# A two-layer relational graph network on one core: bases multiplied over four chunks at once, and rows copied by hand on one DMA queue in place of two

## The chip, the core and the metric

One core of a Trainium2 chip runs the whole kernel in one launch. The metric is device microseconds for that launch. The engines named below are PE (TensorE; its weight loads are listed apart as PEld), DVE (VectorE), ACT (ScalarE), POOL (GpSimd) and SP (SyncE). SP and ACT can each issue plain DMAs on a queue of their own, and POOL issues indirect DMAs (gathers). An engine runs its instructions strictly in the order of its program, DMA issues included.

## What is computed

There are N = 50,000 nodes with 128 features and 850,000 edges, sorted by target node; 50,000 of them are loops of a node to itself. An edge has one of 16 relations, and the weight of a relation is a mix of 8 bases. Two layers of

```python
W = jnp.einsum('rb,bio->rio', w_comp, basis)
agg = jax.ops.segment_sum(h[src], dst * N_REL + rel, num_segments=N_ENT * N_REL).reshape(N_ENT, N_REL, -1)
msg = jnp.einsum('nri,rio->no', agg, W)
h = relu(msg + h @ loop_w + bias)
```

are followed by `layernorm(x + h)`. All is float32.

## The kernel before, in words

**Chunks.** The 800,000 edges that are not loops are cut into tiles of 128 edges, and K = 10 tiles make a chunk: C = 625 chunks in a layer, 1,250 in all. A chunk's targets lie in a run of some 80 successive nodes. The outer loop (line 876) runs over the layers and the loop at line 940 over the chunks. The program is unrolled completely; the order of PE, POOL, DVE and ACT is the order in which the Python code emits instructions, and the order of SP is left to the planner of the framework.

**Gathers.** For a tile, POOL issues one indirect DMA (line 204, called at 950) that fetches 128 source rows of 512 bytes into one of GATHERS = 5 chunk buffers `g`. The first gather of a chunk waits until PE has read the last tile of the chunk five earlier (`read_by`, lines 951 to 957). Gathers of chunk c + 2 are emitted in chunk c, but POOL is an engine of its own and runs as far ahead as the buffers let it.

**Rows by hand.** In chunks with c % 5 = 4 one tile, and in chunks with c % 5 = 1 one other tile, is not gathered by POOL. Its 128 rows are copied one by one, each by a plain DMA of 512 bytes whose address comes from a register (`row_by_row`, line 814, the DMA at 836). SP copies the tile of the first kind and ACT that of the second (`HANDS`, line 806). The register values are loaded 32 at a time (line 828). Copying begins six chunks before the tile is used and is spread over 45 steps, one after nearly every product, so that two to three row copies at a time stand between the other instructions in ACT's program. Eight semaphores serve the plain DMAs of both queues in turn, so a row copy waits for the DMA that had its semaphore eight copies before, on whichever queue that was.

**Products.** For each tile PE multiplies the 128 gathered rows by a one-hot matrix `hot` that sums them per base and per node slot (12 slots, line 979), into PSUM `pa`, five tiles to a bank. DVE copies each full bank to SBUF (`aT`, line 987). Two chunks later `slots` (line 728) multiplies `aT` of one chunk by the eight bases (line 732: eight matmuls with 120 columns of `aT` as the stationary side and 128 columns moving), and DVE spreads the sum over the J = 4 places of a group row (line 737). Three chunks later `to_nodes` (line 757) adds the result into a group of 512 nodes in PSUM (`pn`, line 768).

**Groups.** There are 98 groups of 512 nodes in a layer, one in 6.4 chunks. For each, `from_itself` (line 681) loads the group's own rows (`h_own`, SP), transposes them on PE (line 695), has ACT copy the result to SBUF (`hT`, line 699), multiplies by the bases (line 710), and lets DVE weigh and reduce (lines 717, 725). The loop weights `lw` come from `loop_weights` (line 644) for four groups at a time, again through a copy on ACT (line 678). At the end of a group `finish` (line 785) adds, applies relu or the normalization on DVE and ACT (lines 792, 587, 595), and SP stores. `weights` (line 619) loads relations for four chunks through SP (`rel`, line 623), which DVE compares at line 630. `beside` (line 916) hands out these pieces between the ten products of a chunk.

Of the kernel before, what the change touches and what calls it, by code (L numbers as in the profile page):

```python
# [50 lines left out]
P = 128  # L51
EPR = 850000
ROW = 10
# [19 lines left out]
SP_EVERY = 5  # L73
ACT_EVERY = 5
OFFSETS = 32
EPS = 1e-5
# [7 lines left out]
def tile_rgcn_resnorm(  # L84
# [33 lines left out]
    assert D == P and N >= P and edges.shape[0] == 1 and AT * NR == P and PER * NB * WN <= BANK and AT * PER * NB == WEIGHTS and PER == HALF and S <= P and C >= 4 and M > 0 and N % C == 0 and N % J == 0 and J * D == BANK and RUN - LK // 2 == LIVE and 2 * C <= NG * P and N <= 1 << 16 and E % ROW == 0  # L118
# [10 lines left out]
    ROW_AT = dram.tile([2 * C, 2, P], I32, name="ROW_AT")  # L129
# [310 lines left out]
    def rows_of(j, pool):  # L440
# [18 lines left out]
        def put(of, to):  # L459
# [17 lines left out]
        row_at = pool.tile([P, LIVE], F32, name="real").bitcast(I32)[:, : 2 * P]  # L477
        nc.vector.tensor_scalar(
            row_at[:m], srcf[:m, LIVE - 2 * P :], float(N - 1), float(4 * D), op0=OP.min, op1=OP.mult
        )  # L480
        nc.sync.dma_start(ROW_AT[r0 : r0 + m].rearrange("r t e -> r (t e)"), row_at[:m])
# [63 lines left out]
    def count_up(pool):  # L545
        last = 5 * NG + len(ROWS)
        off = pool.tile([1, C], F32, name="off_all")
        even = pool.tile([1, C], F32, name="even")
# [48 lines left out]
    def chunked():  # L597
        with (
# [7 lines left out]

            def nodes(g):
                return min(GN, N - g * GN) // J
# [10 lines left out]
            def weights(c, n):  # L619
# [9 lines left out]
                is_rel = hp.tile([P, LIVE], F32, name="is_rel")  # L629
# [14 lines left out]
            def loop_weights(g, n):  # L644
# [14 lines left out]
                is_rel = hp.tile([P // 2, 2, P, J], F32, name="is_l", bufs=1)  # L659
                for h in range(2):  # L660
                    nc.vector.tensor_scalar(  # L661
                        is_rel[:m, h].rearrange("k p j -> k (p j)"), rel[:m, h, :], its_rel1[:m], None, op0=OP.is_equal
                    )
                    if h == 0:
                        yield
                po = ps_o.tile([P, BANK], F32, name="po")
                of = po[:, : J * T * NB].rearrange("p (j t) -> p j t", j=J)
                for j in range(J):
                    for h in range(2):
                        nc.tensor.matmul(  # L670
                            of[:, j, :],
                            is_rel[:m, h, :, j],
                            EACH[n][:m, :T, :].rearrange("k t b -> k (t b)"),
                            start=h == 0,
                            stop=h == 1,
                        )
# [4 lines left out]
            def from_itself(g, of, n):  # L681

                m = nodes(g)
                h = sb.tile([P, J, D], F32, name="h_own", bufs=2)
# [43 lines left out]
            def slots(c, k, aT, n):  # L728

                ps = ps_s.tile([P, BANK], F32, name="ps")  # L730
                for b in range(NB):
# [4 lines left out]
                st = sb.tile([P, J, D], F32, name="slots")  # L736
                nc.vector.tensor_tensor(  # L737
                    st[: k * WN],
                    ps[: k * WN, None, :D].to_broadcast([k * WN, J, D]),
                    which[: k * WN, c, :, None].to_broadcast([k * WN, J, D]),  # L740
                    op=OP.mult,
                )
                yield st
# [61 lines left out]
            behind = {}  # L805
            HANDS = ((nc.sync, SP_EVERY, SP_EVERY - 1), (nc.scalar, ACT_EVERY, ACT_EVERY // 2 - 1))

            def by_hand(c):

                if ks(c) < K:  # L810
                    return []
                return [i for i, (_, every, at) in enumerate(HANDS) if c > every and c % every == at]

            def row_by_row(i, c, of):

                engine, every, _ = HANDS[i]
                tile_at = 1 - by_hand(c).index(i)
                row_at = hp.tile([1, P], I32, name=f"row_at{i}", bufs=2)
                nc.sync.dma_start(row_at, ROW_AT[2 * c + 1 : 2 * c + 2, tile_at])
                to = hp.tile([P, D], F32, name=f"by_hand{i}", bufs=2)  # L820
                byte = of.bitcast(U8).rearrange("n d -> (n d)")
                yield to
                steps = every * (K - 1)
                for step in range(steps):
                    for e in range(step * P // steps, (step + 1) * P // steps):
                        if e % OFFSETS == 0:
                            with tc.issue_after(behind[i]) if i in behind else ExitStack():
                                _, offsets = nc.values_load_multi_w_load_instructions(  # L828
                                    row_at[:, e : e + OFFSETS],
                                    engines=[engine.engine],  # L830
# [5 lines left out]
                        behind[i] = engine.dma_start(row, byte[None, ds(offsets[e % OFFSETS], 4 * D)]).ins  # L836
# [39 lines left out]
            for n, of in enumerate((x, H1)):  # L876
# [21 lines left out]
                def sum_up(c):  # L898
                    for all_slots in slots(c, ks(c), aTs.pop(c), n):
                        yield  # L900
                    st[c] = all_slots

                def own_of_all():

                    for g in range(NGR):
                        while now[0] < first(g) - 2:
                            yield
# [7 lines left out]

                def beside(t, c, owning, summing):
# [3 lines left out]
                    if 1 <= t <= 4:  # L920
                        for _ in range(NB // 4):
                            next(summing, None)
                    if t == 4:
                        done(summing)
                        if c == C - 1:
                            done(sum_up(c - 1))
# [3 lines left out]
                    if t == 8 and c > 2:  # L930
                        for g in to_nodes(c - 3, n):
                            assert made[0] > g
                            ending.append(finish(g, n))
# [4 lines left out]
                handed, fetching = {}, {}  # L938
                owning = own_of_all()
                for c in range(C):  # L940
                    now[0] = c
                    if n == 0 and c:

                        next(coming, None)
                        while ready[0] + 1 < len(ROWS) and 2 * min(C, c + FETCH + 5 + max(SP_EVERY, ACT_EVERY)) > ROWS[ready[0] + 1]:
                            next(coming)
                    for to in range(0 if c == 0 else c + FETCH, min(C, c + FETCH + 1)):
                        buffer = (n * C + to) % GATHERS
                        for k in range(ks(to) - len(by_hand(to))):
# [8 lines left out]
                    for i, (_, every, _) in enumerate(HANDS):  # L958
                        to = c + every + 1
                        if to < C and i in by_hand(to):  # L960
                            fetching[i] = row_by_row(i, to, of)
                            handed.setdefault(to, {})[K - 1 - by_hand(to).index(i)] = next(fetching[i])
                    g, others = rows[(n * C + c) % GATHERS], handed.pop(c, {})
# [7 lines left out]
                    aT = aTs[c] = hp.tile([P, NB, S], F32, name="aT", bufs=3)  # L971
                    summing = sum_up(c - 2) if c > 1 else iter(())
                    for k in range(0, K, PER):
# [3 lines left out]
                        for i in range(PER):  # L977
                            if i < m:
                                product = nc.tensor.matmul(  # L979
                                    pa[:, i * NB * WN : (i + 1) * NB * WN],  # L980
                                    others.get(k + i, g[:, k + i, :]),
# [4 lines left out]
                            if i == m - 1:  # L986
                                nc.vector.tensor_copy(  # L987
                                    aT[:, :, k * WN : (k + m) * WN].rearrange("d b (i w) -> d i b w", w=WN),
# [3 lines left out]
                            if k + i < K - 1:  # L992
                                for each in fetching.values():
                                    next(each, None)
# [8 lines left out]
                    if c > 1:  # L1003
                        masks[c - 2] = masks_of(c - 2)
# [6 lines left out]
                masks[C - 2] = masks_of(C - 2)  # L1011
                ended = to_nodes(C - 3, n) + to_nodes(C - 2, n)
                masks[C - 1] = masks_of(C - 1)
                done(sum_up(C - 1))
                ended += to_nodes(C - 1, n)
                for each in ending + [finish(g, n) for g in ended]:
# [192 lines left out]
```

## Time and profile before

| | before |
|---|---|
| runs | 24193.81, 24302.33, 24279.7 us (median 24279.7) |
| the profiled execution | 24193.81 us, of which the span of the profile is 24192.0 us |
| PE busy | 12144.3 us, 50% (mean granted clock 0.706) |
| POOL busy | 11433.6 us, 47% |
| DVE busy | 8248.2 us, 34% |
| ACT busy | 421.3 us, 2% |
| DMA engines | 16% of their time in packets (12.6% for the gathers), 44 GB/s |

The profile counts as busy only what an engine's datapath does. Issuing a DMA, moving a register and waiting are not busy time, so ACT at 2% may still have a queue that is always occupied. In the view of waits a line reads: engine, result and line that waited, `<-` who ended the wait, total us, number, longest. "issue" means that the engine waited for nothing that the profile shows; "remote" means that a semaphore ended the wait, and the record of what raised it is not matched.

### The profile page before, as it was taken

Reading aid. Unit: us, or ns where it says so; the run is one execution under the profiler, and the core shown is the slowest. Engines: PE = TensorE matmul, PEld = TensorE weight load, DVE = VectorE, ACT = ScalarE, POOL = GpSimd, SP = SyncE. Lnnn points to the kernel's source line nnn. Section 1 sums busy time; section 2 is a strip of 40 time slices with the busy share of each in tenths; the row PEclk is TensorE's granted clock in tenths of the full one; section 3 lists DMA queues with packets and bytes.
Section 4 is the critical chain, followed back from the end, with each engine's and each line's share of the span. In section 5 each row is a group of like instructions: output and inputs, shape, how many; then the busy total and the mean of one; then the engine's idle time right before and its main releaser. Section 6 shows DMA issues by size and latency. Waiting matters only on the chain. (4 is left out here: it accounts for less than half of the span.)

```text
span 24192.0 us, 282779 instructions
## 1 busy us (share of the span) xinstructions
PE 12144.3 (50%) x58712; PEld 9484.3 (39%) x58712; DVE 8248.2 (34%) x14006; ACT 421.3 (2%) x896; POOL 11433.6 (47%) x12037
## 2 busy tenths in 40 slices
PE   4554554444444455554544555544555545455455
PEld 3333433333333334443433434333344334333334
DVE  4433433333333333333333333333333333333333
ACT  0000000000000000000000000000000000000000
POOL 4444444444444444444444445444444444444444
PEclk7776767666676777777766777766777767777677
DMA  1111111111111111111111111111111111111111
GB/s 56 48 50 47 47 47 48 42 45 46 45 41 39 41 41 42 41 41 40 41 43 42 45 43 45 43 42 43 43 44 43 42 42 43 42 43 43 41 44 40
DMA packets 654553, 1055.42 MB, mean 44 GB/s; under 512 B 270883, under 2 KB 380439, under 8 KB 652811
## 3 DMA queue, kind: packets, MB, share of 16 engines
q0 software_dynamic: 387680, 794.28, 12.6%
q1 hardware_dynamic: 198426, 225.12, 2.9%
q10 hardware_dynamic: 66704, 17.83, 0.3%
q14 instruction: 1265, 10.35, 0.1%
q8 instruction: 478, 7.83, 0.1%
HBM read 962.55 MB, written 73.59 MB: 43 GB/s over the span
## 5 line engine op out<-in xcount | busy, mean ns | idle before, releaser
L204 POOL DMA_INDIRECT g<-H,src x6002 | 5702.9, 950 | 6243.8 <-PE pa L979 3467.1
L204 POOL DMA_INDIRECT g<-in_x_dram,src x6002 | 5704.8, 950 | 5897.0 <-PE pa L979 3147.5
L979 PE MATMUL pa<-hot,g 128*128 128x96 f32 x24008 | 4904.7, 316 | 2874.4 <-DVE aT L987 2205.9
L979 PEld LDWEIGHTS pa<-hot,g 128*128 128x128 f32 x24008 | 4552.3, 240 | 4437.7 <-DVE aT L987 2321.8
L732 PE MATMUL ps<-basis,aT 128*120 128x128 f32 x20000 | 4241.2, 347 | 937.9 <-DVE slots L737 548.2
L710 PE MATMUL po<-basis,hT 128*128 128x512 f32 x3136 | 2170.8, 781 | 4692.9 <-ACT hT L699 3444.3
L987 DVE COPY aT<-pa 128x480 f32<-128x480 f32 x2500 | 1631.9, 653 | 7622.5 <-remote 4218.4
L732 PEld LDWEIGHTS ps<-basis,aT 128*120 128x120 f32 x20000 | 3545.6, 246 | 1027.1 <-DVE slots L737 586.6
L768 PE MATMUL pn<-slots,own 120*128 120x512 f32 x4128 | 2378.9, 696 | 717.8 <-DVE own L751 624.3
L710 PEld LDWEIGHTS po<-basis,hT 128*128 128x128 f32 x3136 | 585.0, 233 | 4794.0 <-ACT hT L699 3473.3
L717 DVE TENSOR_TENSOR by<-po,lw 128x512 f32<-128x512 f32 x1568 | 1062.0, 685 | 2684.0 <-PE po L710 2397.7
L725 DVE TENSOR_REDUCE ls<-by 128x128 f32<-128x1152 f32 (+1 forms) x784 | 1664.1, 2123 | 34.5
L737 DVE TENSOR_TENSOR slots<-ps,which 120x512 f32<-120x512 f32 x1250 | 857.3, 686 | 1833.3 <-remote 1380.1
L890 DVE TENSOR_TENSOR hot<-fixed,own 128x960 f32<-128x960 f32 x1250 | 1447.0, 1158 | 42.9
L768 PEld LDWEIGHTS pn<-slots,own 120*128 120x128 f32 x4128 | 809.0, 223 | 1243.7 <-DVE own L751 636.0
L630 DVE TENSOR_SCALAR is_rel<-rel,its_rel 128x640 f32<-128x640 uint8 x314 | 182.3, 581 | 2173.4 <-DMA rel<-REL 2088.0
L670 PE MATMUL po<-each,is_l 64*128 64x32 f32 (+1 forms) x800 | 206.0, 419 | 1203.4 <-DVE is_l L661 1167.6
L670 PEld LDWEIGHTS po<-each,is_l 64*128 64x128 f32 (+1 forms) x800 | 193.5, 324 | 1218.9 <-DVE is_l L661 1180.7
L695 PE MATMUL po<-ident,h_own 128*128 128x128 f32 (+1 forms) x784 | 190.3, 333 | 879.1 <-DMA h_own<-H 661.4
L751 DVE TENSOR_SCALAR own<-col,node 120x128 f32<-120x128 f32 x2064 | 543.4, 313 | 6.6 <-PE pn L768 6.6
L635 PE MATMUL fixed<-each,is_rel 128*128 128x64 f32 x3140 | 452.8, 289 | 132.8 <-issue 130.5
L979 PEld LDWEIGHTS pa<-hot,by_hand 128*128 128x128 f32 x992 | 204.4, 217 | 731.9 <-issue 348.9
(134 smaller groups left out, 3117.5 us busy)
## 6 DMA issues: line engine op xcount, KB each, us to landing
by_hand<-in_x_dram ACTq DMA_DIRECT2D x15872, 0.5 KB
by_hand<-in_x_dram SPq DMA_DIRECT2D x15872, 0.5 KB
by_hand<-H SPq DMA_DIRECT2D x15872, 0.5 KB
by_hand<-H ACTq DMA_DIRECT2D x15872, 0.5 KB
g<-in_x_dram,src POOLq DMA_INDIRECT x6002
g<-H,src POOLq DMA_INDIRECT x6002
rel<-REL SPq DMA_DIRECT2D x312, 80.0 KB
h_own<-in_x_dram SPq DMA_DIRECT2D x97, 256.0 KB
```

The costliest lines, as they stand in the source:

```text
L204: return nc.gpsimd.indirect_dma_start(out=to, out_offset=None, in_=of, in_offset=bass.IndirectOffsetOnAxis(ap=idx, axis=0))
L635: nc.tensor.matmul(of[:, :, j * NB : (j + 1) * NB], is_rel[:m, j * P : (j + 1) * P], EACH[n][:m], start=True, stop=True,)
L710: nc.tensor.matmul(hb[:m], hT[:, j, :m], BASIS[n][:, b : b + few, :].rearrange("p b d -> p (b d)"), start=True, stop=True,)
L717: nc.vector.tensor_tensor(by[:m, b : b + few, :], hb[:m].rearrange("p (b d) -> p b d", d=D), lw[:m, j, g % T, b : b + few, None].to_broadc ...
L725: nc.vector.tensor_reduce(ls[:m, j, :], by[:m].rearrange("p b d -> p d b"), AX.X, OP.add)
L732: nc.tensor.matmul(ps[: k * WN, :D], aT[:, b, : k * WN], BASIS[n][:, b, :], start=b == 0, stop=b == NB - 1)
L737: nc.vector.tensor_tensor(st[: k * WN], ps[: k * WN, None, :D].to_broadcast([k * WN, J, D]), which[: k * WN, c, :, None].to_broadcast([k * ...
L751: nc.vector.tensor_scalar(own[:k], col4[:k], node4[:k, c : c + 1], float(-g * GN), op0=OP.subtract, op1=OP.is_equal)
L768: nc.tensor.matmul(sums[g], own, of[:k].rearrange("s j d -> s (j d)"), start=c == first(g), stop=c == final(g),)
L890: nc.vector.tensor_tensor(hot[:, : ks(c)], pm[:, c % Q * K : c % Q * K + ks(c), :, None].to_broadcast([P, ks(c), NB, WN]), own[:, : ks(c), ...
L979: product = nc.tensor.matmul(pa[:, i * NB * WN : (i + 1) * NB * WN], others.get(k + i, g[:, k + i, :]), hot[:, k + i].rearrange("e b w -> ...
L987: nc.vector.tensor_copy(aT[:, :, k * WN : (k + m) * WN].rearrange("d b (i w) -> d i b w", w=WN), pa[:, : m * NB * WN].rearrange("d (i b w) ...
```

## The change

- `HANDS` goes. Only SP copies rows: one tile in each chunk with c % 5 = 4, from eight chunks ahead (in place of six) and over the same 45 steps. ACT copies none; the tiles that it copied are gathered by POOL.
- ACT, in place of DVE, copies `pa` to `aT`.
- `aT` holds four chunks. `slots_of_batch` multiplies them by the bases together: eight matmuls with a basis as the stationary side and 480 columns moving. ACT copies the result to SBUF (`by_slot`), PE turns it back by four transposes, and DVE spreads each as before (`spread_out`). The last five chunks of a layer are done one by one as before.
- What a chunk gives is added to its group six chunks later (`LAG`) in place of three; the groups' own part begins three chunks later accordingly.
- Buffers: `h_own` 1 for 2, `is_rel` 1 for 2, `slots` 4 for 3, `aT` 2 of four chunks for 3 of one; `is_l` is made in the place of what it is made from.

```diff
-SP_EVERY = 5
-ACT_EVERY = 5
+BATCH = 4
+BY_HAND = 5
+EARLY = 3
+LAG = BATCH + 2
...
-                is_rel = hp.tile([P, LIVE], F32, name="is_rel")
+                is_rel = hp.tile([P, LIVE], F32, name="is_rel", bufs=1)
...
-                is_rel = hp.tile([P // 2, 2, P, J], F32, name="is_l", bufs=1)
+                is_rel = rel.bitcast(F32)
...
-                h = sb.tile([P, J, D], F32, name="h_own", bufs=2)
+                h = sb.tile([P, J, D], F32, name="h_own", bufs=1)
...
-                st = sb.tile([P, J, D], F32, name="slots")
+                yield spread_out(c, ps[:, :D])
+
+            def spread_out(c, of):
+
+                k = ks(c) * WN
+                st = sb.tile([P, J, D], F32, name="slots", bufs=BATCH)
                 nc.vector.tensor_tensor(
...
+            def slots_of_batch(c, aT, st, n):
+
+                ps = ps_s.tile([P, BANK], F32, name="ps")
+                for b in range(NB):
+                    nc.tensor.matmul(
+                        ps[:, : BATCH * S], BASIS[n][:, b, :], aT[:, b, :], start=b == 0, stop=b == NB - 1
+                    )
+                    if b < NB - 1:
+                        yield
+                by_slot = sb.tile([P, BATCH * S], F32, name="by_slot", bufs=1)
+                nc.scalar.copy(by_slot, ps[:, : BATCH * S])
+                yield
+                po = ps_o.tile([P, BANK], F32, name="po")
+                for q in range(BATCH):
+                    nc.tensor.transpose(po[:S, q * P : (q + 1) * P], by_slot[:, q * S : (q + 1) * S], ident)
+                    if q == 1:
+                        yield
+                for q in range(BATCH):
+                    st[c + q] = spread_out(c + q, po[:, q * P : (q + 1) * P])
+                    if q == 1:
+                        yield
+                yield
...
-            HANDS = ((nc.sync, SP_EVERY, SP_EVERY - 1), (nc.scalar, ACT_EVERY, ACT_EVERY // 2 - 1))
+            behind = []
 
             def by_hand(c):
 
-                if ks(c) < K:
-                    return []
-                return [i for i, (_, every, at) in enumerate(HANDS) if c > every and c % every == at]
+                return ks(c) == K and c >= BY_HAND + EARLY and c % BY_HAND == BY_HAND - 1
...
-                        behind[i] = engine.dma_start(row, byte[None, ds(offsets[e % OFFSETS], 4 * D)]).ins
+                        behind[:] = [nc.sync.dma_start(row, byte[None, ds(offsets[e % OFFSETS], 4 * D)]).ins]
...
+                def added_in(c):
+
+                    if c < ALONE + 2:
+                        return [c - LAG] if c >= LAG else []
...
-                        while now[0] < first(g) - 2:
+                        while now[0] < min(first(g) + LAG - 5, C - LAG - 2):
...
-                    if 1 <= t <= 4:
+                    if c < ALONE + 2:
+                        if t in (1, 3, 6, 9):
+                            next(summing, None)
+                    elif 1 <= t <= 4:
                         for _ in range(NB // 4):
                             next(summing, None)
...
-                    for i, (_, every, _) in enumerate(HANDS):
-                        to = c + every + 1
-                        if to < C and i in by_hand(to):
-                            fetching[i] = row_by_row(i, to, of)
+                    to = c + BY_HAND + EARLY
+                    if to < C and by_hand(to):
+                        fetching = row_by_row(to, of)
+                        handed[to] = next(fetching)
...
-                    aT = aTs[c] = hp.tile([P, NB, S], F32, name="aT", bufs=3)
-                    summing = sum_up(c - 2) if c > 1 else iter(())
+                    if c % BATCH == 0:
+                        aTs[c // BATCH] = hp.tile([P, NB, BATCH * S], F32, name="aT")
...
-                                nc.vector.tensor_copy(
-                                    aT[:, :, k * WN : (k + m) * WN].rearrange("d b (i w) -> d i b w", w=WN),
+                                nc.scalar.copy(
+                                    aT[:, :, place_of + k * WN : place_of + (k + m) * WN].rearrange(
+                                        "d b (i w) -> d i b w", w=WN
+                                    ),
```

## The prediction

> **What bounds the kernel now.** I first read the page for who is busy. Nobody is: 50% PE, 47% POOL, 34% DVE, 2% ACT.
>
> ```profile
> span 24192.0 us, 282779 instructions
> ...
> L204 POOL DMA_INDIRECT g<-H,src x6002 | 5702.9, 950 | 6243.8 <-PE pa L979 3467.1
> L204 POOL DMA_INDIRECT g<-in_x_dram,src x6002 | 5704.8, 950 | 5897.0 <-PE pa L979 3147.5
> ...
> by_hand<-in_x_dram ACTq DMA_DIRECT2D x15872, 0.5 KB
> by_hand<-in_x_dram SPq DMA_DIRECT2D x15872, 0.5 KB
> ```
>
> POOL's 12,004 gathers and the idle time before them fill the span, so POOL's timeline can be cut up. The waits say by whom it is held, and who holds that one:
>
> ```profile
> POOL g L204 <- PE pa L979: 6614.6, 433, 43.5
> ACT hT L699 <- DMA by_hand<-in_x_dram: 5201.1, 78, 117.5
> ACT hT L699 <- DMA by_hand<-H: 4739.5, 88, 82.4
> DVE aT L987 <- remote: 4218.4, 661, 53.4
> PE po L710 <- ACT hT L699: 3444.3, 144, 64.1
> POOL g L204 <- issue: 3287.0, 10609, 30.5
> DVE is_rel L630 <- DMA rel<-REL: 2088.0, 120, 60.3
> POOL g L204 <- remote: 1804.6, 687, 9.1
> ```
>
> The chain is POOL <- PE <- ACT's copy hT <- row copies. The timelines of ACT, PE and POOL around one such hold:
>
> ```profile
> 12644.48 54.24 ACTq L836 DMA_DIRECT2D by_hand<-H  x71
> 12698.76 0.27 ACT L678 COPY lw<-po 128x128 f32<-128x128 f32 x1 [54.02 <-DMA by_hand<-H]
> 12700.09 11.80 ACTq L836 DMA_DIRECT2D by_hand<-H  x26
> 12711.99 0.59 ACT L699 COPY hT<-po 128x512 f32<-128x512 f32 x1 [12.96 <-DMA by_hand<-H]
> ...
> 12712.62 2.07 PE L710 MATMUL po<-basis,hT 128*128 128x512 f32 x2 [39.20 <-ACT hT L699]
> ...
> 12680.56 0.95 POOL L204 DMA_INDIRECT g<-H,src  x1 [2.51 <-remote]
> 12681.81 0.95 POOL L204 DMA_INDIRECT g<-H,src  x1 [0.30 <-issue]
> ...
> 12691.81 0.95 POOL L204 DMA_INDIRECT g<-H,src  x1 [0.31 <-issue]
> 12722.59 0.94 POOL L204 DMA_INDIRECT g<-H,src  x1 [29.83 <-PE pa L979]
> ```
>
> The reader is to see that ACT is late, not busy: its 0.6 us copy hT stands behind 26 row copies, lw behind 71 at 0.76 us each, and PE and then POOL stand still for 39 and 30 us. ACT's 128 copies per five chunks take 128 x 0.76 = 97 us, and five chunks last 5 x 24192 / 1250 = 96.8 us: this queue is full. So is SP's, which copies as many.
>
> POOL's span in four terms. Gathers follow each other at 12681.81 - 12680.56 = 1.25 us (counted over the trace: 1.2525 us for 10,246 of the 12,003 intervals): 12,004 x 1.2525 = 15,035. At a chunk's first gather the interval is about 3.5 us even where PE had read the buffer 2 to 9 us before ([2.51 <-remote] above; 817 intervals lie between 3 and 5 us): 1,250 x (3.5 - 1.25) = 2,812. Before the first gather and after the last lie 47 + 66 = 113. What remains, 24,192 - 17,960 = 6,232, are the holds: 32 us for each of the 196 groups. The intervals over 5 us agree: 380, in sum 7,588, less 380 x 3.5 = 6,258.
>
> **The change part by part**, against the profiled execution (24,193.8 us, 1.8 us around its span, 0.4% under the median).
>
> 1. Gathers: 248 tiles return to POOL. 248 x 1.2525 = +311 us on the path.
>
> 2. ACT copies no rows. Its 31,744 copies and 992 loads of 32 registers go, and SP loses the 248 loads of `row_at` for them. ACT then has 421 us of today, 2,500 copies aT and 310 copies by_slot; at the 586 ns of hT (512 columns) that is under 1,650 us, some 2,070 of the span's time, 1.7 us per chunk. hT, lw, relu and the normalization come when their inputs do. The holds caused by ACT go: up to -6,232.
>
> 3. What is late next is SP. It keeps its 31,744 copies and stands ahead of rel, h_own, lrel and the stores. Waits of today that end on such a load: 2,088 (rel) + 932 (is_l on lrel) + 661 + 215 (PE on h_own, line 695) = 3,896 us, many beside a hold. How fast SP will be is the open price. From the trace, from the end of one row copy to the end of the next with nothing between: 0.648 us on average where ACT issued one within 2 us (23,446 pairs), 0.536 where it did not (6,908). Of the 0.536, 0.105 is wait for the semaphore of the copy eight back in both queues, which is only about four back on SP; alone SP has all eight, and a landing takes some 1.5 us (the DMAs by_hand of 1.46 and 1.62 us at the end of the chain of waits) against 8 x 0.33. So 0.43 to 0.536 is likely; the lower bound is the 0.325 of the last rows, when POOL is done (24143.79 to 24144.11 in the chain of waits), the upper 0.648. SP's whole work is 31,744 x this + 992 register loads x 1.885 (1,870) + some 1,500 for its other DMAs and waits: 17.0 ms at 0.43, 20.4 at 0.536, 13.7 and 23.9 at the bounds. I take the middle of the likely ones, 0.48 and 18.7 ms, because the rows with ACT silent are the nearest and part of their wait goes.
>
> 4. So POOL without holds, 15,035 + 311 + 2,812 + 113 = 18,271, and SP at 18.7 ms lie together. Neither hides the other: each store makes SP wait for the group's end, and each load of h_own and rel makes PE and DVE wait for SP. I leave a third of the 3,896: +1,250. Bounds: 0, and the SP sum of 23.9 ms.
>
> 5. PE: 20,000 matmuls of line 732 (4,241 us busy, 347 ns) become 4,960 of 480 columns, at 781 x 480/512 = 732 ns from line 710 (3,631), 2,480 of the transposes at 333 ns from line 695 (826), and 160 as before (56): 4,513, so +270, beside POOL's gathers: PE's busy time is 9.7 us per chunk of 14.6. If that cover went, 0.2 us per chunk.
>
> 6. The new chain PE ps - ACT by_slot - PE transposes - DVE spread: PE waits for by_slot once in four chunks with two products between. The nearest rows are DVE's 6.4 us mean wait "remote" for PE's semaphore while POOL gathers (4,218 / 661), and 0.59 us, hT with no wait. It ends within the 2 to 9 us by which PE is early at a chunk's end, so I take 0; exposed it is 310 x 6.4 = 1,984. A gain is excluded, as no such step was there before.
>
> 7. DVE loses line 987 (1,632 us) and its wait for rel no longer holds up aT: nothing, since DVE at 34% hides it; were DVE's wait the bound it would be -1.6 ms. The later adding (LAG) and the smaller buffers move work by three chunks and add no instruction; `h_own` with one buffer can load after the transposes of the group before, 6.4 chunks earlier: 0.
>
> Sum: 24,193.8 + 311 - 6,232 + 1,250 = 19,523; I say 19,500 us, 15.5 us per chunk.
>
> A rule that speaks against this stands in the Trainium skill, "DMA: Bandwidth & Descriptors", section "Issuing engines are not separate DMA queues": issuing from several engines saves only sequencer time, usually small beside the DMA. By it ACT's issues were cheap, dropping them would free next to nothing, and the sum would be 24,194 + 311 = 24,505. In this trace a row takes 0.76 us of ACT and the time is all issue.
>
> **The rivals.**
>
> SP is the bound. For it: its queue is full now and loses not one row. Against it: it shares semaphores with ACT today. At 0.55 to 0.63 us per row: 20.8 to 23.4 ms.
>
> The chunk's first gather waits less. The 2.25 us come while PE is always late; if PE keeps close behind POOL, the wait has ended before. Against it: the interval is 3.5 us also where PE finished 9 us before. Without it: 18,271 - 2,812 = 15,459; with half of it and 0.5 ms of SP's waits, 17.4 ms.
>
> The handshakes bound PE, and it is slower. Each chunk needs two copies pa -> aT before PE may go on, now behind ACT's other work, and DVE's waits for PE's semaphore are 6.4 us where they occur. If both cost that in every chunk: 9.7 + 2 x 6.4 = 22.5 us, 28.2 ms. It decides from (19.35 - 9.7) / 2 = 4.8 us each. Against it: the same two stand there today, and between holds chunks take 14 us.
>
> Nothing changes: PE's hold has another releaser behind hT, such as h_own behind SP's rows, and the pitch stays 19.4 us: 24.2 to 24.4 ms. For it: ACT and SP are equally late now. Against it: only 876 us of waits on h_own.
>
> **How the numbers follow.** My case, 18.3 to 20.8 ms: 0.58. SP the bound, to 23.5: 0.20. The cheaper first gather, 15.5 to 18.3: 0.12. Handshakes, over 24.4: 0.07. Nothing changes: 0.03. Faster 0.90, within 0.5% 0.03, slower 0.07; the three runs differ by 0.45%, so 0.5% is what can be told from no change. The range leaves out the lower half of the third case, the last sixth of the second and the last two: 17,300 to 23,000.
>
> **What would show it.** Right: no wait of ACT hT, lw or ls on by_hand; POOL's idle time down from 12,141 to some 7,500 us, its intervals over 5 us nearly gone and the 3.5 us ones left; SP's copies 0.43 to 0.54 us apart. Wrong: PE or DVE waiting over 4 ms for rel, h_own or by_hand (SP is the bound); aT <- PE or PE <- ACT aT, by_slot in the thousands of us (handshakes); first gathers 1.25 us after the last (the third case). The number fails most easily on the SP row and on the first-gather wait, both taken from a kernel in which two queues are entangled.

## The result, and the profile after

The changed kernel takes 22,685.7 us (median of four runs, 22,663.0 to 22,782.8) against 24,291.0 us before: a ratio of 0.9355, interval [0.9318, 0.9391]. Forecast were 19,500 us. The direction was right and the gain a third of what was forecast: the holds of POOL by ACT's copies went, and holds by SP came.

These times need one remark ahead of all others. Later runs, made in five groups, each on one chip, met chips of two kinds. On the first kind the kernel before takes 24.2 to 24.7 ms, as in all runs on record up to the prediction; on the second the same program takes 17.30 ms, and the changed one 15,496.5 us (0.8957, interval [0.8942, 0.8972]). No run of a group departs from the kind of its chip; as no chip is known to have been met twice, "kind" says here what a group of runs met, and not that a chip keeps it. Unless said otherwise, what follows is the first kind.

The profiled execution took 22,663.0 us. From its page: the span, POOL's groups of gathers and SP's row copies.

```profile
span 22661.2 us, 191120 instructions
...
L206 POOL DMA_INDIRECT g<-H,src x6126 | 5791.7, 945 | 5388.5 <-PE pa L1023 2718.1
L206 POOL DMA_INDIRECT g<-in_x_dram,src x6126 | 5796.8, 946 | 5111.4 <-PE pa L1023 2627.1
...
by_hand<-in_x_dram SPq DMA_DIRECT2D x15872, 0.5 KB
by_hand<-H SPq DMA_DIRECT2D x15872, 0.5 KB
```

POOL's idle time fell only from 12,141 to 10,500 us, where some 7,500 were forecast. The waits of the changed kernel (engine, result and line that waited, who ended it, total us, number, longest):

```profile
ACT aT L1031 <- remote: 9150.3, 820, 38.8
ACT aT L1031 <- PE pa L1023: 6619.3, 955, 52.6
POOL g L206 <- PE pa L1023: 5345.2, 368, 50.1
DVE is_rel L632 <- DMA rel<-REL: 4277.5, 172, 65.9
...
DVE lrel L663 <- DMA lrel<-LREL: 1280.6, 74, 58.0
```

No wait on `by_hand` by ACT is left. In its place stand loads on SP's queue: the wait for `rel` doubled from 2,088 to 4,278 us, that for `lrel` rose from 932 to 1,281. One such hold, from the timelines of SP, DVE, PE and POOL (start, us, engine, line, what; in brackets the idle time before and what ended it):

```profile
12641.58 40.44 SPq L859 DMA_DIRECT2D by_hand<-H  x64
12682.07 0.62 SPq L625 DMA_DIRECT2D rel<-REL  x1
12684.15 0.61 SPq L625 DMA_DIRECT2D rel<-REL  x1
...
12684.56 0.55 DVE L632 TENSOR_SCALAR is_rel<-rel,its_rel 128x640 f32<-128x640 uint8 x1 [37.06 <-DMA rel<-REL]
...
12685.96 2.07 PE L710 MATMUL po<-basis,hT 128*128 128x512 f32 x2 [36.51 <-DVE by L717]
...
12696.33 0.94 POOL L206 DMA_INDIRECT g<-H,src  x1 [33.16 <-PE pa L1023]
```

It is the picture of before with SP in ACT's place: 64 row copies stand ahead of the load of `rel`, DVE waits 37 us, PE 37, POOL 33. SP's queue is full. Its 31,744 rows took 19,487 us of the 22,661 (the copies, the register moves before them and the gaps before both), 0.614 us each; 992 register loads took 1,837, and the rest of its work some 1,340. The waits of SP that the profile shows, of all kinds, come to 752 us.

Why a row costs 0.614 us is seen where the instructions are listed with their shortest, median and longest duration in ns. First the changed kernel on the first kind of chip, then the same program on the second:

```profile
L859 SPq MOVE by_hand<-in_x_dram x15872: 1/29/1425, 52.7 to 11410.7; - x199
L859 SPq MOVE by_hand<-H x15872: 1/29/1399, 11455.2 to 22610.1; - x199
```

```profile
L859 SPq MOVE by_hand<-in_x_dram x15872: 29/29/38, 53.2 to 7725.7; - x199
L859 SPq MOVE by_hand<-H x15872: 29/29/38, 7795.6 to 15426.1; - x199
```

A register move, which transfers nothing and waits for nothing, takes 29 ns (38 at most) on the second kind and up to 1,425 on the first. The mean there is 0.034 us in rows that SP copies while POOL stands and 0.180 while POOL gathers; a whole row takes 0.337 us in the one case (11,754 rows) and 0.788 in the other (18,632). (Counted from the end of one copy to the end of the next, intervals under 3 us; POOL counts as gathering if a gather ended between 1.7 us ahead of that interval and its end; with a stretch of the same length for every row, the last 1.7 us, it is 0.404 and 0.761.) On the second kind a row takes 0.332 us while POOL gathers. The granted clock is lower on the first kind, 0.717 against 0.829 in the changed kernel, but the engines' own work is as fast there: a product of line 1023 takes 313 ns on average against 320, a gather 946 against 948, a copy `aT` 558 against 558.

What counts is how long POOL has gathered. The rows of SP, sorted by the gather beside which the row before them ended (a chain is gathers that start less than 1.6 us apart; beside one means from its start to 0.4 us past its end):

| us per row, intervals of all lengths | first two gathers of a chain | 3rd to 6th | 7th to 10th | later ones | POOL stands |
|---|---|---|---|---|---|
| changed kernel | 0.363 | 0.695 | 1.134 | 2.085 (1,418 rows) | 0.382 |
| the same, second kind | 0.357 | 0.358 | 0.334 | 0.332 | 0.425 |
| kernel before with SP's rows alone | 0.351 | 0.702 | 1.118 | 2.138 (737 rows) | 0.386 |
| changed kernel with half the gathers | 0.343 | 0.631 | 1.125 | 1.867 (74 rows) | 0.332 |

The first two gathers cost SP next to nothing; a row beside the eleventh or a later one costs nearly six times as much. The last two lines are of experiments below.

### The profile page after: what moved, and what is told of

The parts are those of the page before. It is cut to its first block, busy times and chain, and to the rows that moved or that the text cites. A ratio compares the mean times of both kernels' runs of the same rounds, so it can differ in the third digit from the quotient of the medians.

```text
span 22661.2 us, 191120 instructions
## 1 busy us (share of the span) xinstructions
PE 11605.0 (51%) x45072; PEld 7642.6 (34%) x45072; DVE 6712.8 (30%) x11506; ACT 1902.9 (8%) x3706; POOL 11614.3 (51%) x12285
## 5 line engine op out<-in xcount | busy, mean ns | idle before, releaser
L1023 PE MATMUL pa<-hot,g 128*128 128x96 f32 x24504 | 4535.0, 313 | 1929.5 <-ACT aT L1031 1107.3
L754 PE MATMUL ps<-aT,basis 128*128 128x480 f32 x4960 | 3081.3, 707 | 1314.3 <-ACT aT L1031 872.4
L1031 ACT COPY aT<-pa 128x480 f32<-128x480 f32 x2500 | 1375.6, 558 | 17880.7 <-remote 9150.3
L754 PEld LDWEIGHTS ps<-aT,basis 128*128 128x128 f32 x4960 | 924.1, 231 | 1375.4 <-ACT aT L1031 899.6
L742 DVE TENSOR_TENSOR slots<-po,which 120x512 f32<-120x512 f32 x1240 | 780.7, 681 | 1576.4 <-remote 780.6
L906 DVE TENSOR_TENSOR own<-fixed,key 128x120 bf16<-128x120 f32 x1250 | 344.2, 275 | 1887.7 <-remote 1092.0
L764 PE MATMUL po<-ident,by_slot 128*120 128x128 f32 x1240 | 346.6, 375 | 1039.7 <-ACT by_slot L760 798.4
L670 PE MATMUL po<-each,lrel 64*128 64x32 f32 (+1 forms) x800 | 205.8, 416 | 1106.3 <-DVE lrel L663 1052.0
L670 PEld LDWEIGHTS po<-each,lrel 64*128 64x128 f32 (+1 forms) x800 | 193.7, 324 | 1119.1 <-DVE lrel L663 1063.3
L764 PEld LDWEIGHTS po<-ident,by_slot 128*120 128x120 f32 x1240 | 189.7, 193 | 1087.4 <-ACT by_slot L760 831.0
```

Source lines behind the costliest of these rows:

```text
L670: nc.tensor.matmul(of[:, j, :], is_rel[:m, h, :].rearrange("k (p j) -> k p j", j=J)[:, :, j], EACH[n][:m, :T, :].rearrange("k t b -> k (t ...
L742: nc.vector.tensor_tensor(st[:k], of[:k, None, :].to_broadcast([k, J, D]), which[:k, c, :, None].to_broadcast([k, J, D]), op=OP.mult,)
L754: nc.tensor.matmul(ps[:, : BATCH * S], BASIS[n][:, b, :], aT[:, b, :], start=b == 0, stop=b == NB - 1)
L764: nc.tensor.transpose(po[:S, q * P : (q + 1) * P], by_slot[:, q * S : (q + 1) * S], ident)
L1023: product = nc.tensor.matmul(pa[:, i * NB * WN : (i + 1) * NB * WN], g[:, k + i, :] if k + i < ks(c) - by_hand(c) else handed.pop(c), hot[ ...
L1031: nc.scalar.copy(aT[:, :, place_of + k * WN : place_of + (k + m) * WN].rearrange("d b (i w) -> d i b w", w=WN), pa[:, : m * NB * WN].rearr ...
```

## The experiments

The first four kernels ran together, beside a run of the kernel before of 24,201 us.

**No rows, changed kernel.**

```diff
-                return ks(c) == K and c >= BY_HAND + EARLY and c % BY_HAND == BY_HAND - 1
+                return False
```

> The changed kernel with no tile copied row by row: POOL gathers all 12,500. Theory Q (SP's queue of row copies is what bounds the changed kernel: 31,744 x 0.614 us + loads and the rest = its whole span): SP becomes free and POOL bounds: 12,500 x 1.25 = 15.6 ms, plus at most 1,250 x 2.25 = 2.8 ms of first gathers: 16 to 19 ms, and DVE's wait of is_rel for rel (4,278 us) falls under 500. Theory H (handshakes between PE, ACT and DVE bound it, 18 us per chunk): the rows are hidden, and the time stays at 22.3 to 22.9 ms.

**No rows, kernel before.**

```diff
-                return [i for i, (_, every, at) in enumerate(HANDS) if c > every and c % every == at]
+                return []
```

> The kernel before with no tile copied row by row on either queue. Theory Q: the holds of 32 us per group come from the two queues alone; without them POOL's 12,500 x 1.2525 + 2,812 + 113 = 18.6 ms, within 3% of the changed kernel without rows. Theory H (the batch of four chunks and ACT's copies shorten or lengthen the chunk): the two kernels without rows differ by more than 3%.

**Rows of SP alone, kernel before.**

```diff
-            HANDS = ((nc.sync, SP_EVERY, SP_EVERY - 1), (nc.scalar, ACT_EVERY, ACT_EVERY // 2 - 1))
+            HANDS = ((nc.sync, SP_EVERY, SP_EVERY - 1),)
```

> The kernel before with ACT's row copies left out (POOL gathers those tiles) and SP's kept, all else as before. Theory Q: SP alone has the same rows as in the changed kernel, so its queue sets the same time, 22.3 to 23.0 ms, and taking ACT's rows away is the whole of the gain. If the batch, ACT's copies or the eight chunks ahead gave the gain: 23.8 to 24.5 ms. If ACT's rows alone were the hold and SP's rows cost nothing: 18.3 ms.

**Half as many rows, changed kernel.**

```diff
-BY_HAND = 5
+BY_HAND = 10
```

> The changed kernel with a tile copied row by row in every tenth chunk in place of every fifth (over ten chunks, so half as many rows per chunk). Theory Q: SP's work falls to about 15,900 x 0.61 + 2.3 = 12 ms, under POOL's 12,376 x 1.25 = 15.5 ms plus first gathers, so 16 to 19 ms, within 0.5 ms of the kernel with no rows. If SP's loads are late merely because they stand behind rows, even with SP not full, the time lies midway, near 20.5 ms. Theory H: 22.3 to 22.9 ms.

| kernel | us | POOL's gathers |
|---|---|---|
| before | 24,201.2 | 12,004 |
| before, SP's rows alone | 21,840.4 | 12,252 |
| before, no rows | 18,789.0 | 12,500 |
| changed, a row tile in every tenth chunk | 19,253.4 | 12,376 |
| changed, no rows | 18,774.5 | 12,500 |

Without rows both kernels take 14% less than the best of those with rows in every fifth chunk, though POOL then gathers 12,500 tiles. So the rows are the bound and the handshakes are not. Half as many rows leave 0.48 ms of them, just outside 16 to 19 ms but within the 0.5 ms that were expected of a queue of SP that is no longer full. The two kernels without rows differ by 0.1%: the batch of four, the copies on ACT and the later adding are worth nothing there. Dropping ACT's rows alone made 21.84 ms out of 24.20, more than the whole change did; that lies in none of the three ranges, and nearest to the one by which SP's queue sets the time. And 18,775 us are near what the prediction's formula for POOL gives, 18,271 + 248 x 1.25 = 18,581, but the sum hits by luck: of the 1,249 first gathers 603 follow within 1.6 us, 400 come 3 to 5 us after the last one, and 223 later than that, where the formula had 2.25 us for each.

The profile of the changed kernel without rows shows what POOL still waits for. Its waits, and then the timelines of PE, POOL and ACT around one stop:

```profile
ACT aT L1031 <- remote: 8549.9, 755, 43.6
...
POOL g L206 <- PE pa L1023: 1379.9, 245, 15.4
POOL g L206 <- remote: 1378.2, 364, 8.5
```

```profile
12023.17 0.36 PE L1023 MATMUL pa<-hot,g 128*128 128x96 f32 x2
12023.36 1.00 PE L754 MATMUL ps<-aT,basis 128*128 128x480 f32 x2
12032.83 1.17 PE L1023 MATMUL pa<-hot,g 128*128 128x96 f32 x4 [8.47 <-issue]
...
12031.24 0.94 POOL L206 DMA_INDIRECT g<-H,src  x1 [0.30 <-issue]
12036.18 0.94 POOL L206 DMA_INDIRECT g<-H,src  x1 [4.00 <-remote]
...
12032.22 0.56 ACT L1031 COPY aT<-pa 128x480 f32<-128x480 f32 x1 [8.93 <-remote]
```

PE's product ends at 12,023.5, ACT is free, and yet the copy `aT` starts 8.7 us later, at 12,032.22, when POOL's last gather has just ended (12,032.18; half of the late copies start some 2 us or more after one). PE, with two tiles `pa`, stands meanwhile. In this trace 981 of the 2,500 copies `aT` start over 1 us after both PE's product and ACT's earlier work were done, together 9.0 ms; in the changed kernel itself 1,002 do. The recorded updates of PE's semaphore come in bursts 42 or 43 ns apart after a chain of gathers (2,399 such steps here, none in the changed kernel on the second kind). So a chain of gathers holds up PE's semaphores as well as SP's moves, and the first-gather wait, which the prediction took as a constant of 2.25 us per chunk without a reason for it, goes with it: the changed kernel on the second kind shows neither.

The next four ran beside 24,298 us before.

**Half the gathers.** POOL fetches every second tile, PE reads each of them twice; the rows of the other tiles are left out of the sums.

```diff
-                        for k in range(ks(to) - by_hand(to)):
+                        for k in range(0, ks(to) - by_hand(to), 2):
...
-                                    g[:, k + i, :] if k + i < ks(c) - by_hand(c) else handed.pop(c),
+                                    g[:, (k + i) // 2 * 2, :] if k + i < ks(c) - by_hand(c) else handed.pop(c),
```

> The changed kernel with its gathers halved: POOL fetches only every second tile of a chunk, and PE reads each fetched tile twice, so that the output is not the reference's. SyncE's row copies stay as they are, 31,744. Theory G, a row copy is cheap and each gather that runs beside it holds SyncE up: with 12,252 gathers the rows took 19.5 ms, which is 31,744 x 0.33 + 12,252 x 0.73; with half the gathers it is 10.5 + 4.5 = 15.0 ms, 0.47 us per row, and with 3.1 ms of other work SyncE needs 18.1 ms: the time is 17 to 19 ms, or less if gathers stop being dense. Rival, the row copy costs SyncE 0.61 us by itself: the rows keep 0.61 us and the time stays within 22 to 22.7 ms.

16,050.9 us, and 0.407 us per row (12,906 us for the 31,744), with SP's queue still full. The page shows the halved gathers and POOL's idle time:

```profile
span 16049.1 us, 183870 instructions
...
L206 POOL DMA_INDIRECT g<-H,src x3125 | 2975.0, 952 | 4932.6 <-PE pa L1023 3894.3
L206 POOL DMA_INDIRECT g<-in_x_dram,src x3125 | 2974.9, 952 | 4563.1 <-PE pa L1023 3540.2
```

SP's own work was not touched, and its row became a third cheaper: the gathers set its price, and the rival falls. The size was off, and 16.05 ms lie under the 17 to 19 that were expected: against the 0.336 us of a row on the second kind of chip, a gather cost SP (0.614 - 0.336) x 31,744 / 12,252 = 0.72 us in the changed kernel but 0.36 us here (6,250 gathers). It is no constant per gather. Nor is it how densely gathers follow each other, since within a chain they are 1.25 us apart in both. The chains are shorter here, 5.1 gathers on average against 12.1, and by the table above the first gathers of a chain are the cheap ones.

**Loads on ACT's queue.**

```diff
-                nc.sync.dma_start(h[:m], of_group(of, g))
+                nc.scalar.dma_start(h[:m], of_group(of, g))
```

and likewise for `rel`, `lrel` and `xw`.

> The loads of rel, lrel, h_own and xw are issued by ScalarE; SyncE keeps the row copies, their row_at loads and the stores. Theory T, SyncE's throughput is what counts: rows 19.5 ms, register loads 1.84, stores and row_at under 1 ms remain, the loads moved were some 0.5 ms of it; time 21.5 to 22.5 ms, with PE or POOL now waiting for by_hand in place of rel, lrel and h_own. Rival L, the loads stand behind rows and it is their lateness that stops DVE and PE: the 4,278 + 1,281 + 607 us of waits on rel, lrel and h_own go and the time falls under 21 ms.

24,725.3 us: slower than either kernel, and outside both expectations. What SP waits for in this kernel:

```profile
SPq L859 <- DMA rel<-REL: 832.7, 86, 34.1
SPq L859 <- DMA xw<-in_x_dram: 608.1, 35, 28.1
SPq L859 <- DMA h_own<-in_x_dram: 177.5, 14, 33.6
```

SP's row copies now wait up to 34 us for loads that ACT issues: the two queues take the eight DMA semaphores in turn, and a row that is given the semaphore of a load must wait until ACT, late itself, has issued that load and it has landed. The gaps ahead of SP's row copies grew from 3,974 to 8,209 us, a row to 0.70 us, and PE now waits 5,076 us for `by_hand`. Moving DMAs to a second queue took little load off the first, which kept all its rows, and tied the two together. The Trainium skill, "Perfetto Trace Analysis", section "DMA Optimizations", says that balancing DMAs over the engines that can issue them may help where the generation of descriptors is the bottleneck. Here, where an issuing queue is full and four kinds of loads were moved off it, the time rose by 2.0 ms.

**Copies `aT` on DVE again.**

```diff
-                                nc.scalar.copy(
+                                nc.vector.tensor_copy(
```

> The copies pa to aT are on VectorE again, as before the change. Before with SyncE's rows alone took 21.84 ms, the changed kernel 22.69. If the copies on ScalarE are what costs the 0.85 ms: 21.7 to 22.0 ms. If not: 22.5 to 22.9 ms. In the two kernels without rows the place of the copies was worth nothing, so I expect the second.

**Rows begin six chunks ahead again.**

```diff
-EARLY = 3
+EARLY = 1
```

> Rows begin six chunks ahead in place of eight, as before the change. If SyncE's throughput is the bound, rows that begin two chunks later change nothing or leave less slack: 22.5 to 23.2 ms. If the earlier start is what made the changed kernel slower than before with SyncE's rows alone (rows pushed ahead of loads that are due sooner): 21.7 to 22.2 ms, and the wait of DVE on rel falls from 4,278 us to about 2,300.

22,599.8 and 22,609.3 us: neither is why the changed kernel takes 0.85 ms more than the kernel before with SP's rows alone. SP is full in both; what differs is its row, 0.614 against 0.590 us, 0.76 ms over all rows. The table above says where that comes from: beside a gather of the same place in its chain a row costs the same in both kernels, within 4%, but the changed kernel has longer chains, 2,479 gathers behind the tenth of their chain against 1,307, and nearly twice as many rows beside these. With the other kernel's prices its rows would come to 0.619 us where 0.618 was measured, so its rows' places in the chains are the whole difference.

The next four ran on a chip of the second kind, where the kernel before took 17,304.4 us.

**Timed without rows, and a sixth gather buffer.** The edits of the kernels without rows as above; for the third also

```diff
-GATHERS = 5
+GATHERS = 6
```

> The changed kernel with no row copies at all and 12,500 gathers, timed for its interval: one look gave 18,774.5 us, so 18,750 to 18,850 us, some 0.77 of the kernel before.

> The kernel before with no row copies, timed for its interval. If the batch of four chunks, the copies on ScalarE and the later adding are worth nothing where POOL is the bound: 18,750 to 18,850 us, the same as the changed kernel without rows within 0.5%. If they are worth a gain that one look missed by scatter: at least 0.5% above it.

> The changed kernel with no row copies and six buffers for the gathered rows in place of five. 12,500 gathers at 1.25 us are 15.6 ms; some 3 ms of longer intervals are left, most of 4.8 us at every second chunk. If POOL stops there because its buffers are full, a sixth lets it run a chunk further between stops: two stops in six chunks go, and the time falls by 0.3 to 0.9 ms to 17.9 to 18.5 ms. If the stop comes because PE, with two tiles pa, cannot get further ahead of the copies aT while POOL gathers, a sixth buffer changes nothing: 18.65 to 18.85 ms.

**Two buffers `is_rel`**, with the rows.

```diff
-                is_rel = hp.tile([P, LIVE], F32, name="is_rel", bufs=1)
+                is_rel = hp.tile([P, LIVE], F32, name="is_rel")
```

> The changed kernel with two buffers is_rel again, as before the change. It is one of the two smaller buffers that could be why the changed kernel takes 0.85 ms more than before with SyncE's rows alone, and VectorE's wait for rel is 4,278 us here against 2,275 there. If the single buffer is the cause: 21.8 to 22.2 ms. If SyncE's cost of a row is (0.614 against 0.590 us there, and its queue full in both): 22.5 to 22.8 ms, which I expect.

15,803.1 (ratio 0.9132, interval [0.9116, 0.9147]), 15,815.1 (0.9140, [0.9124, 0.9155]), 15,796.8 (0.9131, [0.9115, 0.9146]) and 15,497.7 us. All four miss their expectations by far, because all were written for the first kind of chip. The gathers are no faster here, 1.25 us apart as ever; what is gone are the stops between them. Which of this is the chip and which the edit, the next four runs told.

**The kernels themselves, beside each other**, on another chip (before: 17,302.4 us, again the second kind).

> The changed kernel itself, beside the kernel before on the same chip. If the chip decides: where the kernel before takes 17.3 ms, SyncE's row costs 0.34 us, POOL goes without stops and this takes 15.4 to 15.6 ms (0.89 to 0.90); where it takes 24.2 ms, 22.6 to 22.8 ms (0.93 to 0.94). If the two buffers is_rel of the last look made the difference: 22.6 to 22.8 ms on either chip, or, where before takes 17.3 ms, well above 15.6.

> The kernel before, for its profile on this chip. Where it takes 17.3 ms: copies aT start 0.04 us after PE's product even while POOL gathers, first gathers follow the last at 1.25 us, and what is left above 12,004 x 1.25 = 15.0 ms, 2.3 ms, is rows of ScalarE and SyncE ahead of hT and loads, so that PE stands and POOL with it. Where it takes 24.2 ms: as the first profile, first gathers 3 to 3.5 us after the last and rows of 0.64 us.

> Beside the changed kernel on the same chip: two is_rel are worth nothing, the same within 0.5%. If the single buffer holds VectorE up, this is faster by at least 0.5 ms.

> The kernel before with SyncE's rows alone. Where before takes 24.2 ms it took 21.84 ms against 22.69 of the changed kernel. Where before takes 17.3 ms and a row costs 0.34 us, SyncE is not the bound and POOL's 12,252 gathers are: 15.4 to 15.6 ms, the same as the changed kernel.

15,496.5, 17,297.2, 15,489.6 and 15,513.8 us, as expected if the chip decides. From the page and the waits of the changed kernel there:

```profile
span 15491.8 us, 191120 instructions
...
L206 POOL DMA_INDIRECT g<-in_x_dram,src x6126 | 5816.2, 949 | 1898.4 <-issue 1713.3
L206 POOL DMA_INDIRECT g<-H,src x6126 | 5803.1, 947 | 1885.2 <-issue 1746.2
```

```profile
ACT aT L1031 <- PE pa L1023: 12148.9, 2380, 32.6
POOL g L206 <- issue: 3459.6, 11289, 17.7
...
DVE is_rel L632 <- DMA rel<-REL: 876.8, 114, 30.7
```

POOL no longer waits for PE: its idle time is the 0.3 us of issue between gathers. Of the 12,251 intervals between gathers five are over 3 us, against 904 on the first kind; none of the 2,500 copies `aT` is over 1 us late, against 1,002. The waits of the kernel before on this chip:

```profile
ACT hT L699 <- DMA by_hand<-in_x_dram: 3914.9, 92, 67.2
ACT hT L699 <- DMA by_hand<-H: 3654.1, 95, 59.2
...
POOL g L204 <- PE pa L979: 1850.2, 334, 24.4
...
DVE is_rel L630 <- DMA rel<-REL: 1661.3, 130, 44.4
```

The chain is the one of the prediction, POOL <- PE <- `hT` <- row copies, and the change removes it here without anything in its place. The rows of SP pay here: 15,803 without them less 15,497 with them is 306 us, the 248 gathers saved at 1.25 us, 310 (measured on two chips on which the kernel before differs by 0.01%). The kernel before with SP's rows alone takes 15,514: of the whole change, which saves 1,801 us beside it, dropping ACT's rows is all but 17 us.

**Two of them once more**, for what only the first kind of chip can show; before took 24,683.7 us.

> No row copies, six gather buffers. Where the kernel before takes 24.2 ms: if full buffers stop POOL, 17.9 to 18.5 ms against 18.77 with five; if PE's late semaphores do, since with two tiles pa PE cannot run ahead of the copies aT, 18.65 to 18.85 ms, which I expect. Where before takes 17.3 ms: 15.8 ms, as it was, and nothing is told apart.

> Two buffers is_rel. Where the kernel before takes 24.2 ms: 21.8 to 22.2 ms if the single buffer is what costs the 0.85 ms against before with SyncE's rows alone; 22.5 to 22.8 ms if not, which I expect, since SyncE's queue is full in both. Where before takes 17.3 ms: 15.49 ms, as it was.

19,275.0 and 22,922.5 us, that is 0.781 and 0.929 of before, where five buffers gave 0.776 and one `is_rel` 0.9355. Both times lie above their ranges, on a chip where the kernel before takes 1.6% longer too, so that the ratios are compared, each of single runs. A sixth gather buffer is worth nothing, as expected if POOL's stops come from PE's late semaphores (1,014 copies `aT` late) and not from full buffers. The second `is_rel` is not the 0.85 ms either; that would have been 0.902.

## Why the prediction was wrong, and where it was right

**Point 1** (248 gathers at 1.2525 us): right. It is seen alone on the second kind of chip, 306 us.

**Point 2** (ACT's holds go): right in its mechanism. No wait on `by_hand` by ACT is left on either kind. (ACT's 0.76 us per row were those of one group; over the trace a row takes it 0.647 us, so that its queue was taken for 22.6 of 24.2 ms and not quite full. No term of the sum rests on this; and 19,500 us are 15.6 us per chunk, where 15.5 is written.) On the first kind the size of the gain is hidden by SP. On the second kind it is the whole gain: the same formula from the kernel before there, 17,297 - 15,035 - 113 = 2,149 us of holds, gives 17,297 + 311 - 2,149 = 15,459 with nothing in their place, and 15,492 was measured.

**Point 3** is the step that failed: the price of SP's row, taken as 0.48 us, was 0.614. On 31,744 rows that is 4.25 ms, which brings the 18.7 ms for SP to 22.95, and 22.66 was measured. The range up to 0.648 held it; the choice within it was wrong. The rows of the old trace were split by whether ACT issued copies nearby, on the theory that the wait for shared semaphores makes a row slow, so that it would fall to 0.43 to 0.536 us without ACT. The kernel before with ACT silent shows 0.590, from 0.639. The rows had to be split by POOL. Done in that way, the trace of before gives for SP 0.365 us while POOL stands (13,004 rows) and 0.806 while it gathers (17,289), and the moves 0.028 and 0.173 us. The 0.536 us of the rows with ACT silent are a mixture of the two: about half of them run beside a gather, at 0.69 us, and half beside a standing POOL, at 0.37. What a row costs follows POOL, and the changed kernel still has POOL gathering beside 61% of its rows (57% before). With these two prices the old trace gives SP's time T: (T - 3.37) ms of rows, the share 15.35 / T of it at 0.806 us and the rest at 0.365, must make 31,744 rows, and T is an estimate of 22.1 ms. That could be worked out from the old trace, though two prices are coarse where the chains lengthen.

**Point 4** (+1,250 us for SP's lateness) fell with it. It counted on SP and POOL lying together, at 18.7 and 18.3 ms. SP was the bound, and the intervals over 5 us between gathers hold 6,378 - 366 x 1.25 = 5,920 us; the 3 to 5 us ones hold 1,208, less than the 2,812 forecast for first gathers: 265 of these follow the last gather within 1.6 us (43 before), while the intervals over 5 us stayed as many, 366 against 380.

**Points 5 to 7**: nothing, as forecast, on the second kind and wherever no rows are copied. The kernels with and without batch differ by 0.1% without rows on both kinds. On the first kind with rows there is 0.85 ms left that the changed kernel takes more than the kernel before with SP's rows alone. It goes by way of POOL's longer chains, as said above. The place of the copies `aT`, the early start of the rows and the second `is_rel` are not what lengthens them; the batch itself, the later adding and the single `h_own` were not tried alone, and which of them does stays open.

**The rivals.** SP as the bound, at 0.55 to 0.63 us per row and 20.8 to 23.4 ms, is what happened on the first kind. The cheaper first gather was priced at 15,459 us, and on the second kind 15,496 came, but not by the rival's reason: there 988 of the 1,249 first gathers follow within 1.6 us in the kernel before already, so the chip and not the change took that wait away, and the match is luck. The handshakes did not make it slower than before: the copies are late 1,002 times in the changed kernel, but with 981 late ones and no rows 18.8 ms were left. The sign that the prediction gave for them, `aT` waiting for PE by thousands of us, came on both kinds (12,149 us on the second, where no copy is late): it counts an ACT that has nothing else to do, and tells nothing. The rule of the Trainium skill, "DMA: Bandwidth & Descriptors", section "Issuing engines are not separate DMA queues", that issue time is usually small beside the DMA, would have made 24,505 us. It does not hold here, where a row takes its queue 0.34 to 0.65 us: without ACT's issues the kernel before went from 24.20 to 21.84 ms and from 17.30 to 15.51.

**Which version to keep** depends on the kind of chip. On the first kind the one without rows is best, 18,775 us (0.776 of before); on the second the changed kernel, 15,497, and without rows it is 15,803. To leave the rows out costs 2% on the second kind, to keep them 21% on the first.

## What to carry to other kernels

Before pricing an operation by one neighbour, sort its durations by each engine that could slow it, and by how long that engine has been running: a mean over a trace in which the competitor often stands, or runs in short chains, is too low for a kernel in which it runs through. Many small DMAs are paid by the issuing queue, and loads behind them can become the next bound; moving those loads to a second queue that shares semaphores can couple the two. Where a register move, which waits for nothing, takes 29 ns at one time and 1,425 at another, look for what holds the sequencer before adding up its instructions.

## What was not expected of the hardware

- While POOL issues chains of indirect DMAs, SP's register moves and row copies and PE's semaphore updates are held up on some chips: a move of 29 ns lasts 180 on average and up to 1,425, a row copy 0.79 us in place of 0.34, growing along the chain from 0.36 beside its first two gathers to 2.1 behind the tenth; and of ACT's 2,500 copies that wait for PE 1,002 start late, by 7.8 us on average. After the chain the updates arrive 43 ns apart. SP's loads of 32 registers do not show it (1.85 us on average, 2.14 on the second kind).
- On other chips the same program shows none of it, and the kernel before takes 29% less (17.30 against 24.29 ms) at the same 1.25 us per gather. The runs of the result and three later groups met the first kind, two groups the second. What makes the one or the other, and whether the recording of the profile has a part in it, no run here shows.
